# A four-layer graph network on one core: layer 3 reads 14 of its 50 bins' rows by indirect DMA and makes its output inside the block loop; joined one-hots in layer 0; bn_stats between layers 0 and 1

## The chip, the cores and the metric

The kernel runs on one core of one Trainium2 chip. Its time is the device time of one execution in microseconds (us). TensorE is called PE (PEld is its weight load), VectorE DVE, ScalarE ACT, GpSimd POOL; SP is the sync engine, whose queue issues most of the loads and stores. Each engine runs its own instructions in order; semaphores order the engines among each other. An indirect DMA is issued by POOL: it takes a list of 128 row numbers, one per partition, and fetches one row of a table in DRAM for each.

## What is computed

The graph has 6,250 nodes with 128 features and 206,250 edges, sorted by destination (each node has a loop to itself). Four layers follow each other, each on a normalised copy of `x`, and each added to `x`:

```python
edge_index = jnp.stack([src, dst])
h = jnp.maximum(_layernorm(x, axis=-1), 0.0)
x = x + _L0_gnn_ref(h, edge_index, ...)   # edge attention with one softmax over all edges
h = jnp.maximum(_layernorm(x, axis=-1), 0.0)
x = x + _L1_gnn_ref(h, edge_attr_128, edge_index, ...)   # layer norm, an MLP on every edge
h = jnp.maximum(_layernorm(x, axis=-1), 0.0)
x = x + _L2_gnn_ref(h, edge_index, ...)   # mean over neighbours, two linear maps
h = jnp.maximum(_layernorm(x, axis=-1), 0.0)
x = x + _L3_gnn_ref(h, edge_index, ...)   # graph attention
```

Layer 3 is the one that changes most:

```python
h = (x @ W.T).reshape(N, H, OUT)            # 4 heads of 32
a_src = (h * att_src).sum(-1)
a_dst = (h * att_dst).sum(-1)
alpha = leaky_relu(a_src[src] + a_dst[dst], 0.2)
amax = segment_max(alpha, dst)
ex = jnp.exp(alpha - amax[dst])
w = ex / segment_sum(ex, dst)[dst]
out = segment_sum(h[src] * w[:, :, None], dst).reshape(N, H * OUT) + bias
```

The second loop per node that layer 3 adds is handled apart from the edges (the terms with `al` below).

## The kernel before

**Tiles and bins.** Nodes are cut into 49 blocks of 128 (`NJ`). Edges are sorted into bins of 128 slots: one bin for each pair of a source block and a destination block, and a 50th bin per block for what does not fit into the diagonal one. So each block has 50 bins (`NB`), and about two thirds of the slots hold an edge. `SLD[p, B, field, b]` holds, for slot `p` of bin `b` of destination block `B`, the source's (field 0) or the destination's (field 1) number inside its block plus one, and 0 for an empty slot. `rowA` and `rowB` hold the same numbers in DRAM as rows, by source block and by destination block. `EID` holds each slot's edge number; an empty slot has a number beyond the table.

**Rows by products.** The source rows of a bin are not fetched. `ends` (L605) loads slot numbers with one DMA (broadcast to 128 partitions) and compares them with the partition's number: a 0/1 matrix, the one-hot. PE multiplies it by the block's rows in the SBUF table `T`, which holds every node's row as three bf16 pieces whose sum is the f32 value: three products per bin. `hots` (L619) makes the one-hot the other way round, from `SLD`, to sum messages into destinations.

**Stages.** Sorting and the first norm come first (to about 620 us). Then POOL starts 2,450 indirect DMAs (`gather`, L288, called at L684) that bring edge features into bin order through three buffers `ea`, each group of five followed by a plain store to `attr_b`. They run beside layers 0 and 1. An empty slot is beyond `bounds_check` and is skipped.

- *Layer 0* (L704 to L759): per source block, `logits` makes 50 pairs of narrow products `pe`, from two one-hots per ten bins: `oa` (field 0, three buffers, L712) and `ob` (field 1, through `ends`, eleven buffers, kept for `weighted`). `weighted` makes `pd`, scales it to `hd`, and sums into `pu`.
- *The norms between layers 0 and 1* (L789 to L801): seven chunks of seven blocks. `centred` (L219) and `norm_relu` (L234) use whole-chunk operations of 128x896 on DVE, and `to_table` splits into `T`'s three pieces with five more.
- *Layer 1* (L825 to L894) and *layer 2* (L964 to L992) per block; layer 2's `result` is a generator whose steps are put between the bins' work. It ends with a block's `h` (128 features and 4 + 4 attention terms), split into `T[:, :, A]` with an in-place subtract (L959).
- *Layer 3* (L996 to L1129): see below.
- *A closing loop* (L1131 to L1159): reads the sums `sf` back from DRAM, adds the self term from `T`, divides, adds `b3` and `X`, and stores the output.

**Layer 3's loop.** `first(B)` loads the one-hots of all 50 bins (`obs`, five tiles of ten bins, eleven buffers), makes the source scores `se` (narrow products `ps`, then two reductions), turns them (`pT`, `sT`), runs a segmented maximum along the sorted slots (`run`, a scan), turns back (`pv`), splits in three (`rv`, `rest`), and takes each destination's maximum by 50 products `pm` (`at_end`, then `dm`, `dmp`). `second(B)` takes 20 bins at a time: `ends_dst` and `pg` bring destination terms to the slots, `w` is the exponential; then for each four bins, 12 products `ph` (rows), `msg = ph * w` on DVE, `at` (the one-hot cast to f32 on ACT, three buffers), and four products into `pu`. `store` copies `pu` and writes it to `sf`. The loop is written so that `first(B + 1)` comes before `second(B)`:

```python
state = first(0)
for B in range(NJ):
    following = first(B + 1) if B + 1 < NJ else None
    second(B, *state)
    state = following
```

**Order.** The tile framework places each engine's instructions by its own estimate, so those of `first(B + 1)` and `second(B)` are mixed in one fixed order per engine; it adds semaphores for each overlap of what is read and written, by region of a tile.

Of the kernel before, what the change touches and what calls it, by code (L numbers as in the profile page):

```python
# [9 lines left out]
F32 = mybir.dt.float32  # L10
# [8 lines left out]
D = 128  # L19
# [4 lines left out]
P = 128  # L24
# [8 lines left out]
K = 4  # L33
KM = 12
# [17 lines left out]
def tile_gnn(ctx: ExitStack, tc: tile.TileContext, t: dict, out: bass.AP):  # L52
# [10 lines left out]
    adst = keep.tile([P, NJ, HEADS], F32, name="adst")  # L63
    amax = keep.tile([P, NJ, HEADS], F32, name="amax")
# [143 lines left out]
    def spread(col, w=D):  # L208

        return col[:, :, None].to_broadcast([P, CJ, w])  # L210
# [424 lines left out]
    def fast(inner):  # L635
# [59 lines left out]
        with tc.tile_pool(name="a0", bufs=1) as lay:  # L695
# [5 lines left out]
            with tc.tile_pool(name="c0", bufs=2) as pool, tc.tile_pool(  # L701
# [4 lines left out]
                def logits(A):  # L706

                    bins = bins_of(A)
                    pe = psum.tile([P, NB, 6], F32, name="pe")
                    obs = []  # L710
                    for g, n in chunks(NB, FC):
                        oa = pool.tile([P, FC, P], BF16, name="oa", bufs=3)  # L712
                        r = rowA[A, 0, g : g + n, :]
                        nc.sync.dma_start(oa, bass.AP(tensor=r.tensor, offset=r.offset, ap=[[0, P], [1, n * P]]))
                        nc.vector.tensor_scalar(oa, oa, node1, None, op0=ALU.is_equal)
                        ob = ends(pool, rowA[A], g, n, (1,), bufs=11)
                        obs.append(ob)
                        for i, (B, b) in enumerate(bins[g : g + n]):
                            nc.tensor.matmul(pe[:, g + i, :3], oa[:, i, :], PQ[:, A, 0, :], start=True, stop=True)
                            nc.tensor.matmul(pe[:, g + i, 3:], ob[:, 0, i, :], PQ[:, B, 1, :], start=True, stop=True)  # L720
                    e = pool.tile([P, NB], F32, name="e")
                    nc.vector.tensor_reduce(e, pe, AX.X, ALU.add)
                    nc.vector.scalar_tensor_tensor(e, e, 0.01, e, op0=ALU.mult, op1=ALU.max)
                    nc.vector.tensor_add(e, e, off[:, A, :])
                    m = pool.tile([P, 1], F32, name="m")
                    nc.vector.tensor_reduce(m, e, AX.X, ALU.max)
                    pm = psum.tile([P, P], F32, name="pm", bufs=1)
                    nc.tensor.transpose(pm, m.to_broadcast([P, P]), ident)
                    nc.vector.tensor_reduce(peak[:, A : A + 1], pm, AX.X, ALU.max)
                    nc.vector.tensor_scalar_mul(m, peak[:, A : A + 1], -1.0)  # L730
                    w = pool.tile([P, NB], F32, name="w")
                    nc.scalar.activation(w, e, AF.Exp, bias=m)
                    nc.vector.tensor_reduce(mass[:, A : A + 1], w, AX.X, ALU.add)
                    return obs, w

                def weighted(A, obs, w):
                    bins = bins_of(A)
                    pu = psum.tile([P, 2, D], F32, name="pu")
                    for g, n in chunks(NB):
                        pd = psum.tile([P, 4, D], F32, name="pd", bufs=3)  # L740
                        for i, (B, b) in enumerate(bins[g : g + n]):
                            for k in range(3):
                                nc.tensor.matmul(pd[:, i, :], obs[(g + i) // FC][:, 0, (g + i) % FC, :], T[:, k, B, :D],  # L743
                                                 start=(k == 0), stop=(k == 2))
                        hd = pool.tile([P, 4, D], F32, name="hd")
                        for i in range(n):
                            nc.scalar.activation(hd[:, i, :], pd[:, i, :], AF.Copy, scale=w[:, g + i : g + i + 1])  # L747
                        hl = halves(pool, hd, n, D, "hl", 4)
                        s = pool.tile([P, 4, P], F32R, name="at")
                        hots_from(s, A, 0, g, n)  # L750
                        for i in range(n):
                            nc.tensor.matmul(pu, s[:, i, :], hl[:, i], start=(g + i == 0), stop=(g + i == NB - 1))  # L752
# [36 lines left out]
        with tc.tile_pool(name="a1", bufs=2) as pool:  # L789
            for c in range(NC):  # L790
# [5 lines left out]
                norm_relu(pool, xc, y)  # L796
                d, r = centred(pool, y)
                nc.vector.tensor_mul(d, d, spread(r))
                nc.vector.tensor_mul(d, d, along(gamma))
                nc.vector.tensor_add(d, d, along(beta))  # L800
                to_table(pool, d, c)  # L801
# [101 lines left out]
        with tc.tile_pool(name="b2", bufs=3) as pool, tc.tile_pool(  # L903
            name="b2p", bufs=2, space=bass.MemoryType.PSUM
        ) as psum, tc.tile_pool(name="n2", bufs=2) as npool:
            def result(A, pu):
# [49 lines left out]
                nc.vector.tensor_copy(adst[:, A], h[:, DW:])  # L956
                nc.scalar.copy(T[:, 0, A], h[:, :DW])
# [38 lines left out]
        with tc.tile_pool(name="b3", bufs=2) as pool, tc.tile_pool(  # L996
# [3 lines left out]
            FC, GC = 10, 20  # L1000

            def first(B):

                srcs = list(range(NJ)) + [B]
                obs, ats = [], []
                se = pool.tile([P, HEADS, NB], F32, name="se")
                for half in range(2):
                    ps = psum.tile([P, HB, 3, HEADS], F32, name="ps", bufs=2)
                    for b in range(half * HB, (half + 1) * HB):
                        if b % FC == 0:  # L1010
                            obs.append(ends(pool, rowB[B], b, FC, (0,), bufs=11))
                        nc.tensor.matmul(ps[:, b - half * HB], obs[b // FC][:, 0, b % FC, :],
                                         T[:, :, srcs[b], D:DW], start=True, stop=True)
                    nc.vector.tensor_reduce(se[:, :, half * HB : (half + 1) * HB],
                                            ps.rearrange("p b k h -> p h b k"), AX.X, ALU.add)
# [4 lines left out]
                sT = pool.tile([NB, HEADS, P], F32, name="sT")  # L1020
                nc.scalar.copy(sT, pT)
                dT = pool.tile([NB, P], BF16, name="dT")
                nc.sync.dma_start(dT, rowB[B, 1])
                new = pool.tile([NB, P + 1], F32, name="new")
# [5 lines left out]
                run = pool.tile([NB, HEADS + 1, P], F32, name="run")  # L1030
# [12 lines left out]
                rv = pool.tile([P, NB, 3, HEADS + 1], BF16, name="rv")  # L1043
# [3 lines left out]
                nc.vector.tensor_copy(rv[:, :, 1], rest)  # L1047
                nc.vector.tensor_sub(rest, rest, rv[:, :, 1])
                nc.vector.tensor_copy(rv[:, :, 2], rest)
                at_end = pool.tile([P, NB, HEADS + 1], F32, name="at_end")  # L1050
# [9 lines left out]
                off = pool.tile([P, NB], F32, name="off")  # L1060
# [3 lines left out]

                dm = pool.tile([P, 2 * HEADS], F32, name="dm")
                nc.vector.tensor_copy(dm[:, :HEADS], adst[:, B, :])
                m = dm[:, HEADS:]
# [4 lines left out]
                nc.vector.tensor_copy(amax[:, B, :], m)  # L1072
                dmp = pool.tile([P, 3, 2 * HEADS], BF16, name="dmp")
                for k in range(3):
                    nc.vector.tensor_copy(dmp[:, k], dm)
                    if k < 2:
                        nc.vector.tensor_sub(dm, dm, dmp[:, k])
                return obs, ats, se, dmp

            def second(B, obs, ats, se, dmp):  # L1080
# [3 lines left out]
                for g, n in chunks(NB, GC):  # L1084
# [15 lines left out]
                    for g2, n2 in chunks(n):  # L1100
                        b0 = g + g2
                        ph = psum.tile([P, 4, D], F32, name="ph", bufs=2)
                        at = pool.tile([P, 4, P], F32, name="at", bufs=3)
                        for i in range(n2):
                            b = b0 + i
                            for k in range(3):
# [6 lines left out]
                        msg = pool.tile([P, 4, DW], F32, name="msg", bufs=3)  # L1113
# [9 lines left out]
                store(pool, B, pu, DW)  # L1123
# [6 lines left out]

        with tc.tile_pool(name="c3", bufs=2) as pool:  # L1131
            for c in range(NC):
                acc = summed(pool, [sf], c, DW)

                al = pool.tile([P, CJ, HEADS], F32, name="al")
                nc.vector.tensor_add(al, asrc[:, cols(c), :], adst[:, cols(c), :])
                nc.vector.scalar_tensor_tensor(al, al, 0.2, al, op0=ALU.mult, op1=ALU.max)
                nc.vector.tensor_sub(al, al, amax[:, cols(c), :])
                nc.scalar.activation(al, al, AF.Exp)
                den = pool.tile([P, CJ, HEADS], F32, name="den")  # L1140
                nc.vector.tensor_add(den, acc[:, :, D:], al)
                nc.vector.reciprocal(den, den)
                o = pool.tile([P, CJ, D], F32, name="o")

                def heads(v):
                    return v.rearrange("p j (h o) -> p j h o", h=HEADS)

                def per_head(v):
                    return v[:, :, :, None].to_broadcast([P, CJ, HEADS, HD])

                nc.vector.tensor_mul(heads(o), heads(of_table(pool, c)), per_head(al))
                nc.vector.tensor_add(o, o, acc[:, :, :D])
                nc.vector.tensor_mul(heads(o), heads(o), per_head(den))
                nc.vector.tensor_add(o, o, along(b3))
                nc.vector.tensor_add(o, o, X[:, cols(c), :])
                n = min(CJ, NJ - 1 - c * CJ)
                nc.sync.dma_start(node_rows(out, c * CJ, c * CJ + n), o[:, :n, :])
                if n < CJ:
                    nc.sync.dma_start(out[(NJ - 1) * P :], o[:TAIL, n, :])  # L1159
# [399 lines left out]
```

## Time and profile before

| | us |
|---|---|
| median of 14 runs (lowest, highest) | 7799.04 (7713.98, 7848.4) |
| the profiled execution, its time | 7799.67 |
| its span, first to last instruction | 7797.9 |
| sorting and first norm, to layer 0's start | about 620 to 650 |
| layer 0, to | 2266 |
| norms between layers 0 and 1, to | 2414 |
| layer 1, to | 5535 |
| layer 2, to | 6281 |
| layer 3's block loop, to | 7737 |
| closing loop, to | 7798 |
| last gather of edge rows on POOL | 4520 |

| whole span | PE | PEld | DVE | ACT | POOL |
|---|---|---|---|---|---|
| busy us | 6394.8 | 5357.9 | 6182.7 | 3905.1 | 3130.8 |
| share | 82% | 69% | 79% | 50% | 40% |

The mean granted TensorE clock is 0.915 of full speed over the span. How to read: a stage's time is set by the chain of waits inside it, so the busy shares are taken stage by stage. Idle time of an engine is listed with what ended it. Consecutive instructions of one engine overlap a little at their edges, so the sum of single durations is above the busy time.

### The profile page before, as it was taken

The numbers are of one execution on the slowest core, as the hardware profiler recorded it, in microseconds if no ns is written. First come the engines' busy times: TensorE is split into PE (matmuls) and PEld (weight loads), VectorE is DVE, ScalarE is ACT, GpSimd is POOL, SyncE is SP. The second block draws the span as 40 slices with busy tenths as digits, with TensorE's granted clock in tenths as the row PEclk, the third lists the DMA queues.
The fourth block names the chain that finished last, engine by engine and source line by source line (L and its number), as shares of the span: only waits on it lengthen the run. The fifth ranks groups of instructions, "written<-read, shape, count | busy, mean of one in ns | idle before, by whom it ended". The sixth has DMA issues, their size and how long they took to land.

```text
span 7797.9 us, 184369 instructions
## 1 busy us (share of the span) xinstructions
PE 6394.8 (82%) x70696; PEld 5357.9 (69%) x70696; DVE 6182.7 (79%) x13873; ACT 3905.1 (50%) x9837; POOL 3130.8 (40%) x2961
## 2 busy tenths in 40 slices
PE   5776777777745888889888799999999979999996
PEld 4665666666634666666666567767788879888886
DVE  7996776666778778778777688888877788888887
ACT  3444666666643444444444455555566634434442
POOL 0005888888888788888887810000000000000000
PEclk9887888887868999999999999999999989999998
DMA  1004565555635556656666544444100033333332
GB/s 39 6 6 129 176 179 171 171 174 165 183 109 144 167 166 176 171 165 176 168 169 168 157 130 114 113 112 118 38 2 2 2 105 114 119 117 115 118 119 88
DMA packets 578218, 947.44 MB, mean 122 GB/s; under 512 B 116017, under 2 KB 325677, under 8 KB 577328
## 3 DMA queue, kind: packets, MB, share of 16 engines
q1 hardware_dynamic: 456048, 667.52, 29.8%
q0 software_dynamic: 117600, 266.78, 11.6%
q8 instruction: 562, 9.21, 0.5%
q14 instruction: 328, 2.69, 0.1%
q10 hardware_dynamic: 3680, 1.25, 0.1%
HBM read 816.90 MB, written 172.79 MB: 127 GB/s over the span
## 4 chain that ended last, share of the span: by engine, by line
PE 45%; DVE 23%; DMA 12%; issue 9%; ACT 8%; another core or an unknown queue 3%; SPq 0%; DVEq 0%; ACTq 0%
DMA ends<-rowA 7%; PE pu L1122 6%; PE ph L877 5%; PE pt L882 4%; DMA ends<-rowB 4%; PE pu L983 4%; PE pu L752 4%; PE pd L743 3%; PE ph L1107 3%; PE pd L864 3%; DVE at L622 3%; PE pu L890 3%; PE pT L872 3%; DVE hl L660 2%
## 5 line engine op out<-in xcount | busy, mean ns | idle before, releaser
L286 POOL DMA_INDIRECT ea<-in_edge_attr_dram,EID x2450 | 2837.5, 1158 | 745.6 <-issue 733.8
L622 DVE TENSOR_TENSOR at<-row,SLD 128x512 fp32r<-128x512 bf16 (+2 forms) x1617 | 1051.9, 657 | 262.8 <-PE pu L752 68.6
L864 PEld LDWEIGHTS <-ends 128*128 128x128 bf16 x7350 | 506.0, 100 | 483.5 <-issue 396.5
L882 PE MATMUL pt<-w_L_gnn_phi_w,hT 128*128 128x128 f32 x4900 | 768.5, 289 | 64.2 <-ACT hT L879 32.8
L864 PE MATMUL pd<-T,ends 128*128 128x128 bf16 x7350 | 688.3, 223 | 157.1 <-DMA ends<-rowA 136.4
L743 PE MATMUL pd<-T,ends 128*128 128x128 bf16 x7350 | 709.0, 243 | 111.2 <-issue 51.8
L877 PE MATMUL ph<-sT,w_L_gnn_phi_w 128*128 128x512 f32 (+1 forms) x1274 | 689.2, 623 | 126.9 <-ACT sT L875 77.0
L1122 PE MATMUL pu<-msg,at 128*128 128x132 f32 x4900 | 685.1, 291 | 114.5 <-DVE msg L1115 108.4
L1112 ACT CAST at<-at 128x256 f32<-128x256 bf16 x1225 | 442.9, 403 | 630.8 <-PE pu L1122 620.2
L612 DVE TENSOR_SCALAR ends<-ends,node 128x512 bf16<-128x512 bf16 (+2 forms) x1127 | 501.5, 445 | 316.3 <-DMA ends<-rowA 172.7
L882 PEld LDWEIGHTS pt<-w_L_gnn_phi_w,hT 128*128 128x128 f32 x4900 | 632.5, 193 | 160.7 <-ACT hT L879 88.1
L747 ACT ACTIVATE hd<-pd,w 128x128 f32<-128x128 f32 x2450 | 707.6, 368 | 15.0 <-DVE hl L660 7.5
L752 PE MATMUL pu<-hl,at 128*128 128x256 f32 x2450 | 546.2, 350 | 202.7 <-DVE at L622 46.5
L1122 PEld LDWEIGHTS pu<-msg,at 128*128 128x128 f32 x4900 | 611.0, 196 | 136.2 <-issue 115.5
L875 ACT ACTIVATE sT<-pT 128x512 f32<-128x512 f32 (+1 forms) x637 | 369.9, 581 | 620.0 <-PE pT L872 376.8
L879 ACT ACTIVATE hT<-ph,b 128x512 f32<-128x512 f32 (+1 forms) x637 | 426.6, 670 | 488.6 <-PE ph L877 336.6
L743 PEld LDWEIGHTS <-ends 128*128 128x128 bf16 x7350 | 521.5, 110 | 159.4 <-issue 120.5
L659 ACT CAST hl<-hd 128x512 fp32r<-128x512 f32 (+1 forms) x637 | 384.6, 604 | 464.5 <-PE pu L752 315.8
L752 PEld LDWEIGHTS pu<-hl,at 128*128 128x128 f32 x2450 | 412.0, 228 | 268.3 <-issue 168.7
L659 ACT CAST hl<-msg 128x512 fp32r<-128x512 f32 (+1 forms) x637 | 384.2, 603 | 334.8 <-DVE msg L885 207.7
L870 PE MATMUL pT<-ends_r,xr 128*128 128x512 f32 (+1 forms) x1274 | 537.2, 478 | 7.9 <-DVE ends_r L612 4.3
L983 PE MATMUL pu<-T,many 128*128 128x129 bf16 x7350 | 477.3, 221 | 54.0 <-ACT many L979 52.2
(342 smaller groups left out, 13257.2 us busy)
## 6 DMA issues: line engine op xcount, KB each, us to landing
attr_b<-ea POOLq DMA_DIRECT2D x490, 320.0 KB
ea<-attr_b SPq DMA_DIRECT2D x588, 256.0 KB
ends<-rowA SPq DMA_DIRECT2D x1176, 128.0 KB
oa<-rowA SPq DMA_DIRECT2D x245, 320.0 KB
ends<-rowA SPq DMA_DIRECT2D x245, 320.0 KB
ends<-rowB SPq DMA_DIRECT2D x245, 320.0 KB
ends_dst<-rowB SPq DMA_DIRECT2D x98, 640.0 KB
ea<-in_edge_attr_dram,EID POOLq DMA_INDIRECT x2450
```

Of the source, the lines that this page charges most:

```text
L286: nc.gpsimd.indirect_dma_start(out=to, out_offset=None, in_=table, in_offset=bass.IndirectOffsetOnAxis(ap=idx[:, c : c + 1], axis=0), **more)
L622: nc.vector.tensor_tensor(pairs(to), across_pairs(row1, P, n), along_pairs(at, P, n, P), ALU.is_equal)
L659: nc.scalar.copy(o[:, :n, 0], v[:, :n])
L743: nc.tensor.matmul(pd[:, i, :], obs[(g + i) // FC][:, 0, (g + i) % FC, :], T[:, k, B, :D], start=(k == 0), stop=(k == 2))
L747: nc.scalar.activation(hd[:, i, :], pd[:, i, :], AF.Copy, scale=w[:, g + i : g + i + 1])
L752: nc.tensor.matmul(pu, s[:, i, :], hl[:, i], start=(g + i == 0), stop=(g + i == NB - 1))
L864: nc.tensor.matmul(pd[:, i, :], ob[:, 0, i, :], T[:, k, B, :D], start=(k == 0), stop=(k == 2))
L870: nc.tensor.matmul(pT[:, :n, :], xr[:, 0, k], oa[:, 0], start=(k == 0), stop=False)
L877: nc.tensor.matmul(ph[:, :n, :], w1, sT[:, :n, :], start=True, stop=True)
L882: nc.tensor.matmul(pt[:, i, :], hT[:, i, :], w2, start=True, stop=True)
L983: nc.tensor.matmul(pu, many[:, i, :], T2[:, k, B], start=first and k == 0, stop=last and k == 2)
L1122: nc.tensor.matmul(pu, at[:, i, :], msg[:, i, :], start=(b == 0), stop=(b == NB - 1))
```

## The change

1. *Layer 0*: `oa` goes; one call of `ends` makes both one-hots (fields 0 and 1) with one comparison, in eleven buffers of double size.
2. *Norms between layers 0 and 1*: statistics by `bn_stats` per block on DVE, normalisation by one ACT operation per block; two of the three casts into `T` go to ACT, the third is written by the subtract.
3. *Layer 2*: each block's `h` is also stored to a DRAM table `t3h` (by SP), and the bias `b3` is added to `X` there. At its start, `EID` of bins 36 to 49 is rewritten to node numbers (beyond the table for an empty slot).
4. *Layer 3*: for bins 36 to 49 (`GB = 36`), POOL fetches the 14 bins' rows from `t3h` by 14 indirect DMAs per block into one of two buffers `rows`. Their scores come from the rows, masked by `SLD` with one DVE operation; their message product reads `rows` in place of `ph`. The products `ps` and `ph` and the one-hots of these bins go. Several tiles have fewer buffers (`ends` 8 in place of 11, `at` and `msg` 2 in place of 3, the tiles of the maximum 1 in place of 2); the second piece of `rv` is cast on ACT; `dm` and `amax` are no longer copied.
5. *Output*: `finish` copies `pu` into `acc` and, after each seventh block, makes the output of seven blocks and stores it; the closing loop goes.

The core of the diff:

```diff
@@ layer 0, logits
-                        oa = pool.tile([P, FC, P], BF16, name="oa", bufs=3)
-                        r = rowA[A, 0, g : g + n, :]
-                        nc.sync.dma_start(oa, bass.AP(tensor=r.tensor, offset=r.offset, ap=[[0, P], [1, n * P]]))
-                        nc.vector.tensor_scalar(oa, oa, node1, None, op0=ALU.is_equal)
-                        ob = ends(pool, rowA[A], g, n, (1,), bufs=11)
-                        obs.append(ob)
+                        hot = ends(pool, rowA[A], g, n, (0, 1), bufs=11)
+                        obs.append(hot)
@@ norms between layers 0 and 1
+            def normed(to, v, c, f):
+                st = pool.tile([P, CJ, 6], F32, name="st")
+                for j in range(CJ):
+                    nc.vector.bn_stats(st[:, j], v[:, j])
+                r, low = scales(pool, st, CJ)
+                for j in range(CJ):
+                    nc.scalar.activation(to[:, j], v[:, j], f, bias=low[:, j : j + 1], scale=r[:, j : j + 1])
...
-                norm_relu(pool, xc, y)
-                d, r = centred(pool, y)
-                nc.vector.tensor_mul(d, d, spread(r))
+                normed(y, xc, c, AF.Relu)
+                d = pool.tile([P, CJ, D], F32, name="d")
+                normed(d, y, c, AF.Identity)
                 nc.vector.tensor_mul(d, d, along(gamma))
                 nc.vector.tensor_add(d, d, along(beta))
-                to_table(pool, d, c)
+                nc.scalar.copy(T[:, 0, cols(c), :D], d)
+                nc.vector.tensor_sub(d, d, T[:, 0, cols(c), :D])
+                nc.scalar.copy(T[:, 1, cols(c), :D], d)
+                nc.vector.tensor_sub(T[:, 2, cols(c), :D], d, T[:, 1, cols(c), :D])
@@ layer 2
+            nc.gpsimd.iota(first_i[:, :, : NJ - GB], pattern=[[0, NJ], [P, NJ - GB]], base=GB * P - 1,
+                           channel_multiplier=0)
+            nc.gpsimd.iota(first_i[:, :, NJ - GB :], pattern=[[P, NJ], [0, 1]], base=-1, channel_multiplier=0)
+            nc.vector.tensor_copy(first_f, first_i)
+            nc.vector.tensor_add(first_f, first_f, SLD[:, :, 0, GB:, 0])
+            nc.vector.tensor_scalar(void, SLD[:, :, 0, GB:, 0], 0.0, 2.0 * NP, op0=ALU.is_equal, op1=ALU.mult)
+            nc.vector.tensor_add(EID[:, :, GB:], first_f, void)
...
+                nc.sync.dma_start(t3h[A * P : (A + 1) * P], h[:, :DW])
+                nc.vector.tensor_add(X[:, A], X[:, A], b3)
@@ layer 3
+            fetched = [pool.tile([P, NB - GB, DW], F32, name=f"rows{i}", bufs=1) for i in range(2)]
+            for rows in fetched:
+                nc.gpsimd.memset(rows, 0.0)
...
+                rows = fetched[B % 2]
+                for i in range(NB - GB):
+                    gather(rows[:, i, :], t3h, EID[:, B], GB + i, bounds_check=NP - 1, oob_is_err=False)
...
+                nc.vector.scalar_tensor_tensor(
+                    se[:, :, GB:], SLD[:, B, 0, GB:, 0][:, None, :].to_broadcast([P, HEADS, NB - GB]), 0.0,
+                    rows[:, :, D:].rearrange("p b h -> p h b"), op0=ALU.is_gt, op1=ALU.mult)
...
-                nc.vector.tensor_copy(rv[:, :, 1], rest)
-                nc.vector.tensor_sub(rest, rest, rv[:, :, 1])
-                nc.vector.tensor_copy(rv[:, :, 2], rest)
+                nc.scalar.copy(rv[:, :, 1], rest)
+                nc.vector.tensor_sub(rv[:, :, 2], rest, rv[:, :, 1])
...
-                        ph = psum.tile([P, 4, D], F32, name="ph", bufs=2)
-                        at = pool.tile([P, 4, P], F32, name="at", bufs=3)
+                        if b0 < GB:
+                            ph = psum.tile([P, 4, D], F32, name="ph", bufs=2)
+                        else:
+                            ph = rows[:, b0 - GB : b0 - GB + n2, :D]
+                        at = pool.tile([P, 4, P], F32, name="at")
...
-                store(pool, B, pu, DW)
+                finish(B, pu)
+
+            def finish(B, pu):
+                c, j = divmod(B, CJ)
+                if j == 0:
+                    finish.acc = pool.tile([P, CJ, DW], F32, name="acc", bufs=1)
+                    finish.own = pool.tile([P, CJ, DW], F32, name="own", bufs=1)
+                    nc.sync.dma_start(finish.own, chunk(t3h, c))
+                acc, own = finish.acc, finish.own
+                nc.scalar.copy(acc[:, j], pu)
+                if j < CJ - 1:
+                    return
...
+                nc.vector.tensor_mul(heads(own), heads(own), per_head(al))
+                nc.vector.tensor_add(own[:, :, :D], own[:, :, :D], acc[:, :, :D])
+                nc.vector.tensor_mul(heads(own), heads(own), per_head(den))
+                o = X[:, cols(c), :]
+                nc.vector.tensor_add(o, o, own[:, :, :D])
+                n = min(CJ, NJ - 1 - c * CJ)
+                nc.sync.dma_start(node_rows(out, c * CJ, c * CJ + n), o[:, :n, :])
```

In the changed program the score copy from `rows` is line L1049, the message product L1150, and the gathers are issued from L289.

## The prediction

> **What bounds it now.** I read busy time by stage first, since the whole span (PE 82%, DVE 79%) averages stages with different limits. Columns: stretch, its length, busy us (instructions) of PE, PEld, DVE, ACT and POOL, granted clock, DMA share, GB/s.
>
> ```profile
> core 0: us, PE busy (x) PEld busy (x) DVE busy (x) ACT busy (x) POOL busy (x), PEclk, DMA share, GB/s
> 620.00:2270.00 1650.00, 1206.32 (x14929) 1065.49 (x14927) 1108.19 (x2250) 1053.84 (x3201) 1313.62 (x1216) 0.80 0.57 167
> 2270.00:2415.00 145.00, 11.64 (x79) 8.32 (x80) 132.51 (x169) 24.89 (x39) 119.14 (x102) 0.53 0.33 100
> 6272.00:7737.00 1465.00, 1322.58 (x20048) 1283.20 (x20048) 1265.08 (x3247) 586.61 (x2167) 0.00 (x0) 0.96 0.36 114
> 7737.00:7798.00 61.00, 0.00 (x0) 0.00 (x0) 53.53 (x84) 1.58 (x7) 0.00 (x0) 0.51 0.39 108
> ```
>
> Row 1 is layer 0, row 2 the norms between layers 0 and 1 (DVE busy 132 of 145), row 3 layer 3's block loop, row 4 its closing loop. In layer 3 the first `pu` product runs at 6313.3 and the last at 7735.2: 29.0 per destination block, of which PE is busy 1322.6/49 = 27.0 and DVE 1265.1/49 = 25.8. Both engines are nearly full and POOL is idle. The chain of waits inside one block (start, us, what) shows why:
>
> ```profile
> 6909.08 2.04 PE pu L1122 x16
> 6911.12 0.37 PE ph L1107 x7
> 6911.49 3.05 DMA ends<-rowB
> ...
> 6916.41 0.61 DVE msg L1115
> 6917.02 0.14 issue
> 6917.15 2.04 PE pu L1122 x16
> ```
>
> PE, then one load that lands just too late, then DVE, then PE again: a chain with no long hole. Next, the gathers on POOL that exist today (layer 1's edge rows): their line (ns min/median/max), the last ones in time, and the group within the norm stage.
>
> ```profile
> L286 POOL DMA_INDIRECT ea<-in_edge_attr_dram,EID x2450: 993/1042/2758, 652.2 to 4520.0; - x189
> ```
>
> ```profile
> 4519.98 1.34 POOL L286 DMA_INDIRECT ea<-in_edge_attr_dram,EID  x1 [0.30 <-issue]
> 4521.32 0.58 POOL L686 DMA_DIRECT2D attr_b<-ea  x1
> 4523.31 0.56 POOL L688 DMA_DIRECT2D attr_b<-ea  x1 [1.41 <-DMA ea<-in_edge_attr_dram,EID]
> ```
>
> ```profile
> L286 POOL DMA_INDIRECT ea<-in_edge_attr_dram,EID x87 | 112.2, 1289 | 26.5 <-issue 26.5
> ```
>
> A gather holds POOL for at least 0.99 with 0.30 before it: 1.30 is the fastest spacing of 2450, 1.46 the mean (1.158 + 0.30), 1.59 beside the nearly full DVE of the norm stage. The write at 4523.31 waits for a gather whose instruction ended at 4521.32: landing takes 2.0 more.
>
> **Layer 0.** Two comparisons of 10 bins become one of 20: 245 x (558 + 560) ns go, 245 x 877 (the 128x2560 row of L1088) come, 59 less on DVE; DMA issues stay ten per block. These lines are 3.2% of this stage's chain of waits (1.3 + 1.9), some 50 of 1560; 59/274 of that is 11. Bounds -59 and 0; I take -25, between chain share and whole saving, as DVE also feeds PE.
>
> **The norm stage.** Of 15 full-width DVE operations per chunk (about 1.0 start to start) nine go and 14 bn_stats (0.29) and 14 bn_aggr (0.175) come: 6.0 + 6.5 at most + 0.7 = 13.2, or 11 with the usual 0.07 overlap, against 132.5/7 = 18.9. ACT gets 14 x 0.48 + 2 x 0.95 + 2 x 0.30 = 9.2 and stays under DVE. Seven chunks: -40 to -55; with chunk latency showing, -25. I take -47. Nothing hides it: layer 1 starts on its last result.
>
> **Layer 2.** Per block one bias add (0.29) on DVE, busy 575 of 737 there under PE's 667, and one store of `h` on SP, otherwise empty. The in-place subtract of `h` then waits for that store (1.74 from issue to landing, as `sf` at 7735.85 shows), but five or six one-hots of 0.35 are queued between. If that cover fails, 49 x 1 is lost on DVE and the one-hots behind it. The four index operations (128x686, about 0.8 each) are 3. I take +8, bounds 0 and +50.
>
> **Layer 3.** *Goes:* 14 of 50 bins' products, per block 42 `ph` (24 take 1.34, so 2.3) and 14 `ps` (0.3) on PE; on DVE 0.73 of comparisons, 0.19 of score reduction, 0.60 of casts (one moves to ACT), 0.49 of small copies. *Comes:* 14 gathers on POOL; on DVE a masked score copy (0.25, like the 0.232 of a 128x80 one) and one seventh of the output work (5.3/7 = 0.76). DVE: 25.8 - 2.0 + 1.0 = 24.8. On engine sums alone this would be a gain.
>
> *The wait decides.* There are two `rows` buffers. Block B+2's gathers overwrite what block B's last four message products (L1150) read, so gather 0 waits for the first of them, gathers 4, 8 and 12 for the next; POOL is slower than that, so its train starts at the first. DVE's score copy for B+2 (L1049) waits for all 14. DVE runs in order: in the changed program's order about 24 instructions, 8.9 by these rows, stand between that message product and L1049, and the remaining 15.9 stand behind it: the scan, messages, comparisons, everything up to block B+1's own first gathered message, which starts the next train. PE waits for them at the score transposes, then `pu`; SP's loads wait for PE to free the comparisons.
>
> So a block costs one train plus what is behind it. Train: 0.2 of semaphores + six gathers beside a busy DVE (1.46) + eight beside an idle one (1.30) + 2.0 landing = 21.4; bounds 14 x 1.30 + 2.0 = 20.2 and 14 x 1.59 + 4 = 26. Behind it: 15.9 + idle. Today's block idles 29.0 - 25.8 = 3.2, of which 2.1 is late `ends` loads; buffers fall from 11 to 8 and a hand-off to ACT is added, PE has less to do: 3.4, bounds 1 and 6.5. Block: 21.4 + 19.3 = 40.7, bounds 37 and 47.
>
> *Ends.* Layer 2's last DVE result is at 6280.3; two memsets of 1848 columns (0.69 for 640, so 2.0 each), then 28 gathers in a row (1.37 each, 38.4) and landing: 6325. DVE then has 24.7 queued before the first gathered message, with 4 idle: 6354. Then 47 blocks x 40.7 = 1913; the last block gathers for nobody, 20 (13 message groups at PE's 1.7, less three); then 13 of messages, output arithmetic (4.5) and store (5.3, as 7792.58 to 7797.9). End 8300 against 7797.9: +502. The 61 of the closing loop are inside this.
>
> Sum: 502 - 25 - 47 + 8 = +438 on a span of 7797.9: 8236. That execution took 7799.67, the median of 14 is 7799.04, so 2 is added: about **8240**.
>
> [...]
>
> **Rivals.**
> - *Dear train*: gathers at 1.59 throughout, landing 4 behind 640 KB comparison loads, idle 6: 26 + 22 = 48 a block, 8240 + 7.3 x 47 = 8580. For it: the norm stage's row. Against: DVE stands still for over half of the train. 0.13.
> - *Cheap stall*: spacing 1.30 and nearly no idle behind it: 20.2 + 16.5 = 36.7, 8050. For it: PE loses 2.6 a block and has run ahead during the stall. Against: scan, transposes, ACT copies and `pm` alternate between engines. 0.20.
> - *Hidden gathers* (other side): the train fits into the queue before L1049 and DVE's 24.8 or PE's 24.4 plus idle sets the block: 26, 8240 - 14.7 x 47 = 7550. It decides from a block of 31.4 down, which is where the sum meets 7799: a train of 12, 0.71 per gather. Against: no gather of 2450 came under 1.30. 0.03.
> - *The change doesn't skip what it says*, so empty slots cost as full ones: already in, as layer 1's gathers skip in the same way.
>
> **Numbers.** Forecast (38 to 44 a block) 0.62. The range reaches into the dear and cheap cases: 36.7 and 45 a block, 8050 to 8440. A measurement here tells 0.5% (39 us) from no change: faster 0.04, within 0.01, slower 0.95; the other 0.02 is for what no row shows.
>
> **What would show it.** Right: in layer 3 DVE's largest idle is at L1049, released by the gathers' DMA, 10 to 14 per block; POOL busy some 15 of 41 us; PE 60% busy in place of 90; blocks near 41; the norm stage near 98. Wrong: gathers under 1 us apart, or trains that start before the message products of two blocks earlier; L1049 idle small, blocks near 26.

## The result, and the profile after

| | before | changed |
|---|---|---|
| median of runs, us | 7787.18 (47 runs) | 8549.15 (10 runs, 8417.28 to 8617.2) |
| ratio, 95% interval | | 1.0946 [1.0894, 1.0998] |
| profiled execution: span | 7797.9 | 8580.8 |
| layer 0, first to last product | 1612.3 | 1878.1 |
| norms between layers 0 and 1 | 135.7 | 102.4 |
| layer 1 | 3132.3 | 3087.3 |
| layer 2 | 736.8 | 737.4 |
| layer 3 and the end | 1527.7 | 2122.0 |

The change made the kernel 9.5% slower; 8240 was forecast (5.7%). The ratios, here and below, compare only those runs of a kernel that lie within 1.5% of its fastest, so they can differ from the ratio of the medians. The stages (cut here at the first and last products of each, which sets the bounds a few us apart from the earlier table) say where: layer 3 and the end cost 594 more, and layer 0, forecast 25 shorter, became 266 longer. The busy time by stage of the changed kernel, with the columns of the table shown of before:

```profile
650.00:2531.00 1881.00, 1326.87 (x14749) 1151.27 (x14749) 1067.17 (x1967) 1056.47 (x3186) 1508.46 (x1468) 0.73 0.50 159
2531.00:2630.00 99.00, 0.50 (x2) 0.30 (x2) 73.18 (x272) 56.27 (x128) 81.42 (x70) 0.50 0.33 99
6460.00:8520.00 2060.00, 1306.28 (x16794) 1217.18 (x16794) 1243.51 (x2992) 596.38 (x2141) 716.45 (x687) 0.79 0.29 86
8520.00:8581.00 61.00, 42.30 (x511) 40.08 (x511) 34.60 (x74) 21.76 (x83) 1.56 (x2) 0.86 0.14 41
```

Row 1 is layer 0: DVE's work fell (1108 to 1067), POOL is busy for 80% of it and no other engine for more than 71%, yet the stage grew. Row 2 is the norms and row 4 the end of the last block. Row 3 is layer 3: PE 63%, DVE 60%, POOL 716/49 = 14.6 per block. What ended DVE's idle time there (us in total, times, longest), from the list of waits:

```profile
DVE de L1125 <- remote: 234.1, 56, 10.4
DVE se L1046 <- remote: 163.7, 25, 9.7
DVE se L1049 <- DMA rows<-t3h,EID: 93.8, 15, 12.2
DVE msg L1150 <- remote: 53.7, 20, 3.7
```

L1049, where the forecast put the whole wait (10 to 14 per block), comes third with 93.8/49 = 1.9. The first two wait for products of PE (`pg`, `ps`), and are put down to "remote": the update that released them came so long after the product that no instruction fits. One block of the timeline shows it. A train of 14 gathers runs on POOL from 7641.5 to 7659.6:

```profile
7642.57 0.65 PE L1123 MATMUL pg<-dmp,ends_dst 128*128 128x24 bf16 x20
7643.19 2.02 PE L1157 MATMUL pu<-msg,at 128*128 128x132 f32 x16
7645.04 0.17 PE L1044 MATMUL ps<-T,ends 128*128 128x12 bf16 x1
7647.25 0.66 DVE L1125 TENSOR_REDUCE de<-pg 128x160 f32<-128x480 f32 x1 [3.26 <-remote]
...
7651.09 1.22 PE L1157 MATMUL pu<-msg,at 128*128 128x132 f32 x4 [5.88 <-issue]
...
7652.10 0.33 PE L1044 MATMUL ps<-T,ends 128*128 128x12 bf16 x5
7652.28 1.55 PE L1142 MATMUL ph<-T,ends 128*128 128x128 bf16 x13
...
7661.45 0.29 DVE L1046 TENSOR_REDUCE se<-ps 128x44 f32<-128x132 f32 x1 [9.57 <-remote]
```

The 20 `pg` products end at 7643.2 by their records; the reduction that waits for nothing else starts at 7647.25. PE then issues nothing for 5.9 us. The last `ps` products are at 7652.4, and their reduction starts at 7661.45, 1.8 after the train's end. So during the train PE hardly serves DVE, and the work in front of L1049 (8.9 by the forecast) isn't done under the gathers' cover but behind them. Over the 46 blocks from the fourth on: period 42.6, train 18.5 from first issue to last end, and L1049 on average 4.6 after that (up to 2 in 13 of the blocks, over 6 in 23).

The trace's own records of semaphores, counted over the whole run, say the same of PE alone (late: more than 0.1 us after the end of an instruction of that engine that updates it; some records of updates are missing in the first, second and fourth rows, so the shares there are good to about two points):

```
                  a gather begun in the 4 us before   none begun
                  PE          DVE     ACT             PE, DVE, ACT
before            47% late    0%      0%              0%
changed           55% late    0%      0%              0%
e1 (set A)         0% late    0%      0%              0%
e13 (set D)       73% late    0%      0%              0%
```

This is so in the kernel before too, in layers 0 and 1, where its edge gathers run. It stood in its profile as a wait that a program on one core can't have (layer 0's score reduction; busy and mean ns, then idle time and what ended it):

```profile
L722 DVE TENSOR_REDUCE e<-pe 128x50 f32<-128x300 f32 x49 | 23.0, 470 | 200.6 <-remote 169.1 <-PE pd L743 22.2 <-PE pe L720 9.3
```

### The profile page after: what moved, and what is told of

Read it like the earlier page. It is cut to its first block, busy times and chain, and to the rows that moved or that the text cites. A ratio compares the mean times of both kernels' runs of the same rounds, so it can differ in the third digit from the quotient of the medians.

```text
span 8580.8 us, 180866 instructions
## 1 busy us (share of the span) xinstructions
PE 6557.9 (76%) x67952; PEld 5432.4 (63%) x67952; DVE 6074.9 (71%) x13534; ACT 3983.3 (46%) x9984; POOL 3778.9 (44%) x3651
## 4 chain that ended last, share of the span: by engine, by line
PE 38%; issue 19%; DVE 18%; DMA 8%; ACT 6%; another core or an unknown queue 6%; POOL 4%; SPq 0%; DVEq 0%; POOLq 0%; ACTq 0%
DMA ends<-rowA 6%; PE pd L742 5%; PE pu L751 5%; PE pt L892 4%; PE ph L887 4%; POOL rows L289 4%; PE pu L1008 3%; PE pu L900 3%; PE pd L874 3%; PE pT L882 2%; PE pu L1157 2%; DVE hl L663 2%; DVE at L625 2%; PE pT L880 2%
## 5 line engine op out<-in xcount | busy, mean ns | idle before, releaser
L289 POOL DMA_INDIRECT ea<-in_edge_attr_dram,EID x2450 | 2763.5, 1128 | 745.7 <-issue 732.7
L289 POOL DMA_INDIRECT rows<-t3h,EID x686 | 714.8, 1042 | 1332.8 <-DVE msg L1150 862.8
L1157 PE MATMUL pu<-msg,at 128*128 128x132 f32 x4900 | 770.4, 312 | 386.4 <-DVE msg L1150 183.1
L1157 PEld LDWEIGHTS pu<-msg,at 128*128 128x128 f32 x4900 | 684.8, 216 | 424.1 <-issue 384.7
L742 PE MATMUL pd<-T,ends 128*128 128x128 bf16 x7350 | 784.1, 258 | 148.7 <-issue 89.0
L874 PEld LDWEIGHTS <-ends 128*128 128x128 bf16 x7350 | 505.1, 100 | 442.9 <-issue 349.0
L874 PE MATMUL pd<-T,ends 128*128 128x128 bf16 x7350 | 687.0, 223 | 119.5 <-DMA ends<-rowA 102.4
L751 PE MATMUL pu<-hl,at 128*128 128x256 f32 x2450 | 619.8, 383 | 191.5 <-DVE hl L663 73.5
L615 DVE TENSOR_SCALAR ends<-ends,node 128x512 bf16<-128x512 bf16 (+4 forms) x1078 | 557.4, 517 | 244.0 <-DMA ends<-rowA 179.5
L742 PEld LDWEIGHTS <-ends 128*128 128x128 bf16 x7350 | 556.4, 118 | 208.1 <-issue 159.6
L751 PEld LDWEIGHTS pu<-hl,at 128*128 128x128 f32 x2450 | 472.6, 256 | 278.6 <-issue 127.1
```

Source lines behind the costliest of these rows:

```text
L289: nc.gpsimd.indirect_dma_start(out=to, out_offset=None, in_=table, in_offset=bass.IndirectOffsetOnAxis(ap=idx[:, c : c + 1], axis=0), **more)
L615: nc.vector.tensor_scalar(r, o, node1, None, op0=ALU.is_equal)
L742: nc.tensor.matmul(pd[:, i, :], obs[(g + i) // FC][:, 1, (g + i) % FC, :], T[:, k, B, :D], start=(k == 0), stop=(k == 2))
L874: nc.tensor.matmul(pd[:, i, :], ob[:, 0, i, :], T[:, k, B, :D], start=(k == 0), stop=(k == 2))
L1157: nc.tensor.matmul(pu, at[:, i, :], msg[:, i, :], start=(b == 0), stop=(b == NB - 1))
```

## The experiments

The runs came in five sets, and the sets differ: where PE's signals are on time, the kernel before takes 7181 to 7186. Each set ran on one chip, with the numbers 11, 2, 0, 0 and 15 on record for A to E (none for the first pair). C and D bear the same number and behave in opposite ways, and the record doesn't tell whether that is one chip at two times or two chips in different machines. So whether the chip, its machine or the time makes the difference stays open, and the text speaks of sets. "Apart" and "joined" are layer 0's one-hots.

| set | before, median | runs | signals of PE beside gathers | layer 0 apart | layer 0 joined | layer 3's block with gathers |
|---|---|---|---|---|---|---|
| first pair | 7787 | before, changed | late | 1612 | 1878 | 42.6 |
| A | 7181 | e1 to e4 | on time | 1105 | 1063, 1063 | 40.2 |
| B | 7846 | e5 to e8 | late | 1686, 1699 | 1827, 1994 | 42.5 |
| C | 7186 | e9 to e12 | on time | 1100 to 1105 | 1062 | 40.0 |
| D | 9162 | e13 to e16 | late | 3125 | 2442 | 43.4 to 43.9 |
| E | 7814 | e17, e18 | late | 1575 | 1838 | 42.5 |

Layer 2 took 734 to 738, the norms 101 to 103 (changed) or 135 to 137 (before) and a block of layer 3 in the kernel before 29.1 to 29.4 in every set that has a trace of it: the sets differ only where gathers run.

**e1: layer 0's one-hots apart again.**

```diff
-                        hot = ends(pool, rowA[A], g, n, (0, 1), bufs=11)
+                        oa = pool.tile([P, FC, P], BF16, name="oa", bufs=3)
...
+                        ob = ends(pool, rowA[A], g, n, (1,), bufs=11)
```

> The changed kernel with layer 0's two one-hots made apart again, as before; all else as changed. Theory O (the joined one-hot is what made layer 0 longer: 1881 us from 650 to 2531 in the changed kernel's profile against 1650 before): layer 0 back near 1650, the whole time 8549 - 235, some 8315. Rival C (layer 0 was longer for another reason, such as the granted clock of that execution, 0.73 against 0.80): layer 0 stays within 50 of 1881 and the time near 8550.

7606.19 against 7181.06: 1.0586 [1.056, 1.0612]. Layer 0 took 1105, which neither theory had; joined it takes 1063 in e2 and e3 of the same set. So here the joined one-hot saves 42, and theory O is wrong for this set. The stages of e1, layer 0 and layer 3:

```profile
650.00:1757.00 1107.00, 974.59 (x14744) 884.61 (x14745) 1066.65 (x2209) 1032.90 (x3185) 915.13 (x758) 0.99 0.73 211
5617.00:7570.00 1953.00, 1274.70 (x16815) 1203.55 (x16815) 1240.62 (x2999) 597.29 (x2148) 717.08 (x688) 0.81 0.31 91
```

Layer 0's code is that of before, and its DVE work too; here DVE is busy for 96% of it, and the granted clock is 0.99. Layer 3's waits (L1053 is the changed kernel's L1049):

```profile
DVE se L1053 <- DMA rows<-t3h,EID: 503.7, 48, 13.0
DVE ends L615 <- DMA ends<-rowB: 43.1, 61, 1.9
```

10.5 per block at the score copy, released by the gathers' DMA, as forecast, and no "remote".

**e2 and e3: layer 3's gathers left out; gathers that nobody reads.**

```diff
# e2
-                    gather(rows[:, i, :], t3h, EID[:, B], GB + i, bounds_check=NP - 1, oob_is_err=False)
# e3
-                rows = fetched[B % 2]
+                rows = fetched[0]
-                    gather(rows[:, i, :], t3h, EID[:, B], GB + i, bounds_check=NP - 1, oob_is_err=False)
+                    gather(spare[:, i, :], t3h, EID[:, B], GB + i, bounds_check=NP - 1, oob_is_err=False)
```

> The changed kernel without layer 3's 686 gathers: rows stays zero, so 14 bins of each block carry no source rows or scores; all else is issued as before. If the gathers are the whole loss in layer 3 (blocks of 42.6 us in the changed kernel): blocks near 27 (DVE's 24.8 and 2 to 3 idle), 47 x 15.6 = 730 less, some 7820. If fewer buffers and the new order cost too: blocks above 31, over 8000.

> The changed kernel with layer 3's gathers going to one spare tile that nobody reads, and the scores and messages of those 14 bins made from a tile of zeros: POOL issues all 686 gathers, and nobody waits for one. Theory W (the loss is the wait for the landing behind the train): blocks near 27 throughout, some 7820. Theory S (while POOL issues gathers, PE's results reach the other engines late, whoever reads the gathers): the gathers run in one stream of about 686 x 1.3 = 890 us; blocks above 33 during it and near 27 after it, 100 to 200 more than in e2.

6991 and 7003, one run each; blocks 28.2 and 28.4. The expected 7820 was built from the first pair, and this set is faster throughout. In this set theory W holds: the gathers cost what is waited for (40.2 - 28.3 = 12 a block) and next to nothing else; the stream of unread ones cost 12 in all. And without any gathers the 14 bins' missing work makes a block 28.3, against 29.2 before: with the changed kernel's order and buffers there were never more than about 0.9 x 49 = 44 us to gain.

**e4: edge gathers left out.** The call of `gather` on `ea` goes; the stores stay.

> The changed kernel without the 2450 gathers of edge rows that run beside layers 0 and 1 (their stores stay, so layer 1 reads zeros as edge features). Theory S: layer 0 with its joined one-hots falls far below the 1650 of before, to 1150 to 1350 (ACT's 1056 busy and some idle), with PE's signals on time; the joined one-hot costs because its order has more handovers from PE on the path. Rival (the joined order is slow by itself): layer 0 stays above 1600 without gathers.

Layer 0 took 1172, longer than the 1063 with gathers: the stores, no longer held up by gathers, all ran in its first half (the last ended at 1265 us), and the blocks took some 25 until then and 21.2 after; that the stores are what cost it was not shown. In a set with signals on time this tells nothing of theory S.

**e5 to e8: another set.**

> The kernel before, for its trace beside the others. In the first four runs PE's signals (its updates of its semaphore) came 0.014 us after the product's end throughout, and before took 7181; in the two profiles of the measured pair they came up to 11 us late wherever POOL issued gathers, and before took 7799. Theory S2 (late signals are what the two machines differ in, and they cost time only in stages with gathers): if signals are on time here, layer 0 takes near 1100, layer 1 near 3005, the other stages what they took in the pair's profile within 15 each (layer 3 near 1456 + 61), some 7180. If they are late: 1600 and 3120, some 7790.

> The changed kernel itself. If PE's signals are on time (theory S2): layer 0 near 1057 as in e2, layer 3's blocks near 40.2 as in e1, 7606 - 40 = 7566, a ratio of 1.053. If they are late: layer 0 near 1880, blocks near 42.6, 8550, a ratio of 1.095. Rival to S2 (the joined one-hot costs by itself): layer 0 above that of before in both cases.

> The change without its gathers: bn_stats between layers 0 and 1, the stored table and the output inside the loop as in the changed kernel, layer 0 with its two one-hots apart, layer 3 with all 50 bins by products and its old numbers of buffers. Both theories: norm stage -47, the closing loop's 61 replaced by 5.3 more per seventh block on DVE (37) and a tail of some 13: 7181 - 47 - 61 + 37 + 13 = 7123 with signals on time, 7730 with late ones; faster than before by about 0.8%.

> As e3 (layer 3's gathers go to a tile that nobody reads). With signals on time again no cost: blocks near 28.4 during the stream of gathers and after it. With late signals, theory S: blocks above 33 during the stream (about 890 us) and near 28 after it, and layer 0 near 1880; the rival (late signals are a matter of the recording alone and cost nothing): 28.4 throughout.

Signals were late again. e5: 7850, layer 0 1686. e6: 8590.59, 1.1065 [1.0949, 1.1182]; layer 0 1827, blocks 42.5. e8, the kernel of e3, took 8857 in place of 7003. Busy time in 200 us of layer 3 beside the stream of gathers and 200 behind it, first of e3, then of e8:

```profile
5780.00:5980.00 200.00, 174.65 (x2451) 167.64 (x2448) 177.62 (x430) 85.81 (x312) 158.26 (x138) 0.92 0.48 135
6580.00:6780.00 200.00, 175.97 (x2476) 168.87 (x2476) 178.08 (x437) 87.09 (x317) 0.00 (x0) 0.92 0.35 106
```

```profile
6740.00:6940.00 200.00, 18.04 (x72) 10.41 (x72) 4.14 (x8) 1.76 (x7) 152.81 (x154) 0.50 0.16 37
7480.00:7680.00 200.00, 156.47 (x2210) 150.42 (x2211) 157.26 (x375) 78.39 (x285) 0.00 (x0) 0.87 0.29 88
```

In e3 the stream changes next to nothing (2451 products beside it, 2476 behind it). In e8 PE issues 72 products in 200 us beside it and 2210 behind it; the first block took 815 us, the later ones 28. The timeline of e8 inside the stream:

```profile
6900.36 0.27 PE L1143 MATMUL ph<-T,ends 128*128 128x128 bf16 x1 [2.53 <-issue]
6900.40 1.00 POOL L289 DMA_INDIRECT rows<-t3h,EID  x1 [0.31 <-issue]
6901.70 1.00 POOL L289 DMA_INDIRECT rows<-t3h,EID  x1 [0.30 <-issue]
6901.76 0.10 PEld L1143 LDWEIGHTS <-ends 128*128 128x128 bf16 x1 [2.70 <-issue]
6903.00 1.00 POOL L289 DMA_INDIRECT rows<-t3h,EID  x1 [0.30 <-issue]
6903.17 0.27 PE L1143 MATMUL ph<-T,ends 128*128 128x128 bf16 x1 [2.54 <-issue]
```

One instruction of PE, load or product, every 1.40 us, waiting for nothing that the profile shows, while gathers go out every 1.30. Nobody reads these gathers, so this is no wait in the program: theory S holds in this set, and far more strongly than "above 33". The stores of edge rows don't run here, so gathers alone suffice. Nor does the loading of instructions look like the cause: from 6900 to 6921 us the queues for it moved no packet, and PE kept to its 1.40. The rival, a matter of recording alone that costs nothing, falls: layer 3 itself takes 2331 in place of e3's 1438.

e7, the change without layer 3's gathers, took 7693.17 against 7846.14: 0.9854 [0.9734, 0.9973], an interval that nearly reaches 1. Its edit to the changed kernel's layer 3 takes the gathers, `rows` and the score copy out, and puts `ends` back to eleven buffers and `at` and `msg` to three; layer 2 loses the index operations.

**e9 to e12: edge gathers begun later.**

```diff
+        def fetch_edges(after):
...
+            for ea in fetched:
+                nc.gpsimd.tensor_copy(ea[:, 0, 0:1], after)
...
+                    if A == 20:
+                        fetch_edges(peak[:, A : A + 1])
```

> The changed kernel with the edge gathers begun only when block 20 of layer 0 has its peak (POOL waits for it), so that one layer holds blocks without gathers and with them. Theory S2 where PE's signals are late (the joined one-hot costs only beside gathers): blocks 1 to 19 at 21.3 us as on the machine with signals on time, blocks from 23 on at 36 to 40 and uneven; the joined one-hot is then cheaper by 0.7 a block without gathers and dearer by some 5 with them, compared with e10. Rival (the joined order is slow on that machine by itself): its blocks 1 to 19 are above those of e10. Where signals are on time: 21.3 throughout.

> The same delay in the kernel before. Theory S2 with late signals: blocks 1 to 19 of layer 0 at 22.1, from 23 on at 32 to 35 and uneven. Layer 1 may wait for its last edge rows. Where signals are on time: 22.1 throughout.

> As e7, for a second interval (0.9854 there): 0.98 to 0.99 of before.

> e7 with the edge gathers begun after block 10 of layer 0. If PE's signals are late and S2 holds: ten blocks at 22.1 in place of some 34, about 120 less than e11. If they are on time: within 30 of e11, or some more if layer 1 runs into its last edge rows.

(The edit shown is that of e9 and e10. e11 is e7 once more, and e12 is e7 with the same edit at `A == 10`.) Signals were on time: layer 0's blocks took 21.2 to 21.4 (joined) and 22.0 to 22.3 (apart) from the third to the last but one, whether gathers ran or not. e9 and e10 (7733 and 7295) ended late since layer 1 ran into its last edge rows (blocks of 70 to 86 in place of about 61). e11: 7078.39 against 7186.12, 0.9844 [0.9825, 0.9863]; e12 the same, 0.9846 [0.9829, 0.9863]. Layer 3's loop of e11:

```profile
5612.00:7020.00 1408.00, 1264.86 (x19450) 1217.51 (x19451) 1258.03 (x2997) 592.33 (x2146) 0.00 (x0) 0.96 0.38 120
```

PE and DVE are both at 89 to 90% (before, in the first pair, 90 and 86%). Of the gain of 108, 34 are in the norms and 57 to 65 at the end of layer 3, where the closing loop went (against e10 and the first profile); e7's 0.8% was too low an expectation.

**e13 to e18: is it the joined one-hot?**

> The changed kernel once more. With PE's signals on time: 40 less than e14 (layer 0's blocks 21.3 against 22.1), 7566, a ratio near 1.053 to before. With late signals: layer 0 near 1850, the time 150 to 300 above e14, a ratio near 1.10.

> The changed kernel with layer 0's one-hots apart (as e1). With signals on time: 7606, 1.0586. With late signals: layer 0 near 1680, some 8350, a ratio near 1.07. Rival to the joined one-hot as the cause of layer 0's loss: within 60 of e13 with late signals.

> As e9 (edge gathers begin after block 20 of layer 0, joined one-hots). With late signals: blocks 1 to 19 at 21.3, from 23 on uneven and 36 to 40. With signals on time: 21.3 throughout, as in e9.

> As e10 (the same in the kernel before). With late signals: blocks 1 to 19 at 22.1, from 23 on uneven and 32 to 35. With signals on time: 22.1 throughout, as in e10.

> The changed kernel. With PE's signals on time: layer 0's blocks 21.3, layer 3's blocks near 40.0, about 7566, a ratio near 1.053 to before. With late signals: a ratio anywhere from 1.03 to 1.11, since layer 0's length beside gathers is then not set by the form of its one-hots; layer 3's blocks 42 to 44.

> The kernel before on the same chip, for its trace. With signals on time: layer 0 about 1100 (blocks 22.1), layer 1 about 3005, layer 3 as ever (blocks 29.2), 7185. With late signals: layer 0 from 1600 up.

Set D had the most late signals (73% in e13): before took 9162.34, e13 9255.18 (1.0307 [1.0127, 1.0486]), e14 9749.5 (1.0739 [1.0405, 1.1073]). There the joined one-hot was 683 shorter in layer 0, not longer: the expectations for e13 (1850) and e14 (1680, and a shorter time than e13's) fell. Set E was like B: e17 8537.55, 1.0883 [1.0787, 1.0979], layer 0 1838; e18's 1575.

The late start is the cleanest test, since one layer of one execution holds both cases. Four stretches of layer 0 of e16 (12 gathers go out first, then POOL waits 441 us, to 1109), and behind them two of e15:

```profile
720.00:900.00 180.00, 159.63 (x2460) 146.74 (x2460) 175.98 (x368) 172.22 (x532) 0.00 (x0) 1.00 0.53 154
900.00:1080.00 180.00, 160.26 (x2472) 147.47 (x2470) 175.86 (x369) 172.07 (x532) 0.00 (x0) 1.00 0.53 155
1200.00:1380.00 180.00, 109.50 (x1001) 90.12 (x999) 72.95 (x147) 70.35 (x216) 143.14 (x145) 0.58 0.46 137
1380.00:1560.00 180.00, 102.54 (x986) 84.86 (x986) 74.63 (x151) 69.59 (x212) 143.72 (x144) 0.62 0.45 134
```

```profile
900.00:1080.00 180.00, 164.96 (x2579) 149.96 (x2579) 178.05 (x337) 176.55 (x553) 0.00 (x0) 1.00 0.52 160
1200.00:1380.00 180.00, 110.29 (x1089) 93.59 (x1089) 80.38 (x150) 80.36 (x243) 144.26 (x141) 0.63 0.46 140
```

In e16 without gathers PE issues 2460 products in 180 us and DVE is busy for 98%; with them 1000 products, DVE 41%, and the granted clock falls from 1.00 to 0.6. By blocks: 22.0 each up to the eighteenth, then 25 to 101, on average 51.5. In e15 21.2 each, then 29 to 88, on average 51.8 (32 to 35 and 36 to 40 were expected). So without gathers both forms run in this set just as in A and C, and the joined one is 0.8 a block cheaper; with gathers both are some 2.4 times slower and uneven, and the mean tells no difference between the forms.

## Why the prediction was off

**The direction and most of layer 3 were right.** In set A, with layer 0 as before, the changed kernel takes 7606 - 7181 = 425 more, 5.9%; the forecast without its layer 0 term is 438 + 25 = 463. The changed kernel itself never ran as it is in such a set; from e1 and the 42 of layer 0 it would be some 7564, 1.053 (an estimate from those rows).

Of the 783 that the profiled span grew, 438 were forecast. The other 345 are 291 in layer 0, 92 in layer 3 and its end and 14 in the norms, less 45 in layer 1 and 7 in layer 2.

**The step that failed is "Layer 0": "Bounds -59 and 0; I take -25".** Measured: -42 where PE's signals are on time, +266 in the first pair, +142 and +263 in B and E (e6 against e5, e17 against e18), and -683 in D. These are single traces: e6 and e8 have the same layer 0 and set, and differ by 167. The step costed DVE's comparisons and took layer 0 as a stage that its engines' work sets. Beside gathers, where signals are late, it isn't: without them e16 runs it at 22.0 a block (the whole layer took 1100 in e10), with them at 51.5, and the pair's profile has 1612 in all. The clue lay in the window that the prediction itself showed (POOL busy for 1314 of 1650, no other engine above 73%, a clock of 0.80) and in the 169 us of waits for "remote", which it didn't show. What makes the joined form the worse one in all four of its runs in B, E and the pair (1827 to 1994 against 1575 to 1699) and the better one in D stays open, and with it the size of the +266: beside gathers, the blocks of e14 alone range from 27 to 157 us, and e13 to e16 tell only that the form doesn't settle it.

**Layer 3, block by block.** The forecast of 40.7 was one train of 21.4 and 19.3 behind it. Set A: 18.5 + 1.7 to L1053 = 20.2, and 19.9 behind it: 40.2 (rounded). The wait's place, its cause and its size (10.5 per block, forecast 10 to 14) are as written, and POOL's 14.6 of 40 (15 of 41) and PE's 65% (60%) near it. In the pair the block is 42.6, 1.9 x 47 = 89 more than forecast, and that is the 4.6 in place of 2.0 from the train's end to L1049, less 0.9 of a shorter train (and 0.2 more behind it): the assumption that failed is that 8.9 of DVE's work would be done under the train. In the block shown, PE issued nothing for 5.9 of the train's 18. The start held (first gathered message 78 after layer 2's last DVE result, forecast 74), and so did the tail (15 from the last block's first gathered message to the end, forecast 13).

**The other terms.** Norms: -33 for -47; the stage's ACT operations stand in a chain with DVE's (which waits 17 for them), and 73 of 99 us of DVE's busy time is left, near the low bound of -25. Layer 2: +1 for +8, its cover held. Layer 1: -45 in the pair, not forecast; in B and E -25 and -4. In all three the gathers end 62 to 76 earlier, as more of them had run beside the longer layer 0; that this is what shortens layer 1 isn't shown.

**The rivals.** *Dear train* (48 a block, 8580) has nearly the measured time by luck, for a wrong reason: gathers stayed 1.34 apart ((18.5 - 1.04)/13) and in set A landed in 1.7. *Hidden gathers*: e2 and e3 show what it would have been worth, 28.3 a block, not 26; the removed products were only partly on the path. *Cheap stall* (36.7) is excluded by all sets. The range ended at 8440 since it was built from rows of gathers alone; what gathers do to another engine was not among its bounds.

**What stays open.** Why PE is held beside gathers in some sets and not in others. Records go missing in the same stretches: of DVE's semaphore updates the kernel before has a record for 1253 of 2169 in layer 0 and for all 1747 in layer 1 after the last gather, and e1 for 2151 of 2168 in layer 0. No run here was made without records: nothing here shows that recording holds PE, or that it doesn't.

## What to carry to other kernels

Before pricing an edit in a stage, ask whether its engines' work sets that stage at all: if none is near full, find what holds them (here a wait for "remote" in a program that has no remote), since an edit's own cost then says nothing of the stage. In the sets with late signals a gather costs more than its issue and its landing, even when nobody reads it (e8's layer 3: 2331 in place of e3's 1438): what you mean to do under its cover must be shown to run there, on the engine that has to do it. And take the sure part of a change alone: with layer 3's gathers left out, the statistics, the inner output and the small edits that came with them made this kernel 1.5% faster in both kinds of set (0.9844 [0.9825, 0.9863] with signals on time, 0.9854 [0.9734, 0.9973] with late ones).

## What the runs showed of the hardware

- In three of the five sets and in the first pair, PE is held while POOL issues indirect DMAs: down to one instruction per 1.40 us (e8), its signals up to 11.4 us late (55% of them over 0.1 us) in the changed kernel's profile; of DVE's and ACT's signals beside gathers 0% are over 0.1 us late in the four traces counted. In sets A and C nothing of this is seen: 0% of PE's signals are late in e1, and layer 0's blocks take the same with and without gathers in C (21.2 to 21.4 joined, 22.0 to 22.3 apart).
- The same kernel, before, took from 7181 to 9162 us in these sets. Where it was traced (first pair, B, E; in C and D with the late start alone), its norms, layer 2 and layer 3 take the same within 10 us, so what differs lies in the two layers beside gathers.
- Where PE is held, its granted clock falls too (0.58 and 0.62 in e16 beside gathers, 1.00 without; 0.50 in e8's stream), and its products are recorded longer: `pd` in e16 has a mean of 219 ns from 720 to 1080 us and of 276 from 1200 to 1560.
- A train of 14 gathers takes 18.3 to 18.5 us to issue in every set, and in set A 1.7 more to land.
